# Fixing SyncE's order in a group-norm attention kernel, with loads and broadcasts tied to TensorE's progress

## Chip, cores and metric

One core of one Trainium2 chip runs the whole kernel. The metric is the device time of the program in microseconds, the median of three runs: 1814.81 us before the change (1812.54 to 1816.59).

## What is computed

The input x is 32 images of 256 channels and 32 x 32 places, all in 32-bit floats. The reference, cut to what matters:

```python
def _gn(v, G=32, eps=1e-5):           # group norm: 32 groups of 8 channels, no affine part
    ...
def attention(x):                      # xf: [b, 256, 1024]
    q = einsum('oc,bcs->bos', q_w, xf) + q_b
    kv = einsum('oc,bcs->bos', kv_w, xf) + kv_b
    k, v = kv[:, :256], kv[:, 256:]    # 8 heads of 32 channels
    mask = tril(ones(S, S), -1)        # strictly causal: a place sees only earlier ones
    scores = einsum('bhqd,bhkd->bhqk', q, k) / sqrt(32)
    scores = where(mask == 0, -10000, scores)
    attn = where(mask == 0, 0, softmax(scores))
    return einsum('bhqk,bhkd->bhqd', attn, v)
out = x + attention(_gn(x))
```

## The kernel before

The kernel goes through the 32 batches one after the other. A batch is worked in two groups of four heads (g), and each group in six "visits". So a batch has N = 12 visits, and the whole kernel has 384. In each visit TensorE makes scores for four heads (keys on partitions, queries along the free axis), ScalarE takes their exponentials, GpSimd masks the diagonal blocks, TensorE multiplies the exponentials of the visit before with the values, and VectorE adds exponentials up so that the softmax's sums can be formed later. Between these stand pieces of other batches' work: the projections of the next batch, the group norm of the one after, the division and the output of the one before.

Which piece stands at which visit is written out by hand. `when(i, f, where)` puts a function into one of three lists, and the main loop calls them at visit i: `at` after the scores have been issued, `between` after the values, `after` at the end of the visit. The tables PROJECT, PREPARE, SUMS, LOADS and FINISH hold the visit numbers, counted from the first visit of the batch concerned. The context `tc.manual_schedule(engines=...)` keeps this written order for the engines that it names: TensorE, ScalarE, VectorE and GpSimd. SyncE isn't among them, so the planner of the framework chooses the order of SyncE's instructions. SyncE does nothing but issue DMAs, and its queue is in order: an instruction that waits for a semaphore holds all behind it.

SyncE's DMAs in a batch, 256 KB each but for the inverses (32 KB):

- Four loads of x (`load_part`, L107), for the batch two later, quarter by quarter (two groups of channels, two halves of the places). Four buffers of x are kept; a buffer comes free when the batch that used it has been finished by VectorE.
- Four stacks (`stack`, L450): before each, GpSimd's queue folds a tile of partial sums twice with adding DMAs (`fold`, L444: 128 rows to 64 and 64 to 32, 512 KB and 256 KB in the profile's counting), and the stack copies the 32 rows into the tile `folded`. That tile has one buffer, which VectorE's `sum_folded` frees.
- One store of the inverses to DRAM (`invert`, L498), and four broadcasts of these from DRAM into the tile `rb`, 32 partitions for each head (`spread_inverses`, L505, at visits 8 to 11 of the next batch in the table). `rb` has one buffer.
- Four stores of the output (`finish`, L538). `finish` first multiplies the numerators with `rb` on VectorE (L530), adds bias and x (L532), writes the result into `rb` itself, and stores that.

The semaphore `bank_free` is already there. In `scores`, the last matmuls of the first part of a visit's scores each add one to it (four for a visit), and TensorE waits for the running total `live["free"]` before it writes the same banks of PSUM a second time:

```python
for ins in ends:
    ins.then_inc(bank_free, 1)
...
live["free"] = live.get("free", 0) + len(ends)
wait = nc.tensor.wait_ge(bank_free, live["free"])
```

The functions that the change touches and what calls them:

Of the kernel before, what the change touches and what calls it, by code (L numbers as in the profile page):

```python
# [14 lines left out]
ENG = mybir.EngineType  # L15
# [5 lines left out]
HALF = 512  # L21
# [11 lines left out]
def tile_norm_attention_residual(  # L33
# [19 lines left out]
    nc = tc.nc  # L53
# [4 lines left out]
    NH = S // HALF  # L58
# [6 lines left out]
    x_out = out.rearrange("b (g p) h w -> b p g (h w)", p=P)  # L65
# [15 lines left out]
        out=avg, in_=avg, pattern=[[-CPG, P // CPG], [0, CPG]],  # L81
# [3 lines left out]
        out=avg, in_=avg, pattern=[[CPG, P // CPG], [0, CPG]],  # L85
# [13 lines left out]
    def unshifted():  # L99
        live = {}  # L100
        bank_free = tc.alloc_semaphore("bank_free")
        xpool = tc.alloc_tile_pool(name="xpool", bufs=4)

        def load_part(b, g, cols):
            if (g, cols.start) == (0, 0):
                live["x", b] = xpool.tile([P, NG, S], F32, tag="x", name=f"x_{b}")
            nc.sync.dma_start(out=live["x", b][:, g, cols], in_=x_in[b, :, g, cols])  # L107
# [59 lines left out]
        def blocks(tokens, s, turned=False):  # L167

            of = tokens.rearrange("p (n s t) -> p n s t", s=2, t=P)[:, :, s, :]
            return of[:, :, ::-1] if turned else of  # L170
# [275 lines left out]
        def stack(b, n):  # L446
            if n == 0:
                live["folded", b] = work.tile([P, 4, HALF], F32, tag="folded", bufs=1, name=f"folded_{b}")
            total = live.pop(("sum", b, *divmod(n, NH)))
            nc.sync.dma_start(out=live["folded", b][n * HD : (n + 1) * HD], in_=total[:HD])  # L450
# [38 lines left out]
        def invert(b):  # L489
# [9 lines left out]
                out=spread.rearrange("a n j (m c) -> (n j m) a c", c=HD), in_=turned.rearrange("p (a c) -> p a c", a=2),  # L499
            )  # L500

        def spread_inverses(b, h):
            if h == 0:
                live["rb", b] = work.tile([P, 4, HALF], F32, tag="rb", bufs=1, name=f"rb_{b}")
            nc.sync.dma_start(  # L505
                out=live["rb", b][h * HD : (h + 1) * HD],
                in_=live["spread", b][h // 2, :, h % 2, :].unsqueeze(0).broadcast_to([HD, 4, HALF]),
            )
# [13 lines left out]
                inv.unsqueeze(2).broadcast_to([P, k, HD]),  # L522
            )

        def finish(b, n, within=slice(0, HALF)):
            g, hf = divmod(n, NH)
            cols = slice(hf * HALF + within.start, hf * HALF + within.stop)
            num, rb, xt = live["num", b, n], live["rb", b][:, n, within], live["x", b]
            num = num[:, within]
            nc.vector.tensor_mul(num, num, rb)  # L530
            for s in range(2):
                nc.vector.scalar_tensor_tensor(  # L532
                    blocks(rb, s), blocks(num, s, s == 1), v_bias_col[:, g : g + 1], blocks(xt[:, g, cols], s),
                    ALU.add, ALU.add,
                )
            if cols.start == 0:
                nc.vector.tensor_copy(rb[:, 0:1], xt[:, g, 0:1])
            nc.sync.dma_start(out=x_out[b, :, g, cols], in_=rb)  # L538

        def end_last(b):  # L540

# [27 lines left out]
        N, TOTAL = NG * len(VISITS), 2  # L569
# [40 lines left out]
        at, between, after = {}, {}, {}  # L610

        def when(i, f, where=at):
            where.setdefault(i, []).append(f)
# [15 lines left out]
        PROJECT = (-5, -4, -3, -2, -1, 0, 1, 2, 3, 4, 5, 6)  # L629
        PREPARE = (-12, -11, -9, -9, -8, -8, -7, -6, -5, -3)  # L630
        SUMS = (3, 7, 10, 13)
        LOADS = (7, 8, 11, 12)
        FINISH = (N + 13, N + 13, N + 14, N + 16)
        every = range(4)

        with tc.manual_schedule(engines={ENG.PE, ENG.Activation, ENG.DVE, ENG.Pool}):


            load_weights()
            if B > 1:  # L640
                load(1)
            junk = small.tile([P, 1], F32, tag="most", name="junk")
            nc.scalar.activation(junk, ones, AF.Exp)
            keep_busy(16)
            for g in range(NG):
                norm_channels(0, g)
            norm_mean(0)

            live["less_mean"] = work.tile([P, 4, HALF], F32, tag="folded", bufs=1, name="less_mean")[:, 0, :]
            for s in range(2):  # L650
                nc.scalar.activation(
                    blocks(live["less_mean"], s), blocks(live["x", 0][:, 1, :HALF], s, s == 1), AF.Identity,
                    bias=live["minus_mean", 0][:, 1:2],
                )
            turn_weights(0)
            norm_deviation(0)
            norm_variance(0)
            norm_rstd(0)
            for hf in range(NH):
                for g in range(NG):  # L660
                    norm_apply(0, hf, g)
                if hf == 0:
                    for n in (1, 2):
                        turn_weights(n)
                    keep_busy(3)
                    nc.vector.tensor_scalar_mul(qk_bias[:, 0, :], qk_bias[:, 0, :], SCALE)
            units = projections(0)
            for n, f in zip((None, None, None, 0, 0, 0) + PROJECT[6:], units):
                if n is None:
                    f()  # L670
                else:
                    when(n, f)
            if B > 1:
                prepare(1, (None, None, 0, 1, 2, 2, 3, 4, 5, 7))
            for b in range(B):
                first, last = b * N, b == B - 1
                if b >= 1:
                    for n, f in zip(PROJECT if not last else PROJECT[:-1] + (7,), projections(b)):
                        when(first + n, f)
                if b >= 2:  # L680
                    for n in range(NG * NH):
                        cols = slice(n % NH * HALF, (n % NH + 1) * HALF)
                        when(max(first - 2 * N + LOADS[n], 0), lambda b=b, n=n, cols=cols: load_part(b, n // NH, cols))
                    prepare(b, [(first + n,) if k in (2, 3) else first + n for k, n in enumerate(PREPARE)])
                if not last:
                    for n in every:
                        v = first + SUMS[n]
                        when(v, lambda b=b, n=n: fold(b, n, 2 * HD), after)
                        when(v + 2, lambda b=b, n=n: fold(b, n, HD), after)
                        when(v + 4, lambda b=b, n=n: stack(b, n))  # L690
                    late = b == B - 2
                    v = first + N + (5 if late else 6)
                    when(v, lambda b=b: sum_folded(b, every[:2]), after)
                    when(v + 1, lambda b=b: sum_folded(b, every[2:]), after)
                    when(v + 2, lambda b=b: invert(b))
                    for n in every:
                        when(v + 2 + (0 if late else n), lambda b=b, n=n: spread_inverses(b, n))
                    for n in every:
                        v = first + (N + 9 + n // 2 if late else FINISH[n])
                        when(v, lambda b=b, n=n: finish(b, n), after)  # L700
                else:
                    when(first + 3, lambda: sums(0, SUMMED[1], False), after)
                    when(first + 7, lambda: sums(1, SUMMED[5], False), after)
                    when(first + 9, lambda: sums(2, SUMMED[7], False), after)
                    when(first + 8, lambda b=b: invert_here(b, 0))
                    when(first + 9, lambda b=b: finish(b, 0))
                    when(first + 8, lambda b=b: invert_here(b, 1))
                    when(first + 8, lambda b=b: finish(b, 1))
                    when(first + 10, lambda b=b: invert_here(b, 2))
                    when(first + 11, lambda b=b: finish(b, 2), after)  # L710
            for i in range(B * N + 1):
                if i < B * N:
                    scores(*divmod(i, N))
                for f in at.pop(i, ()):
                    f()
                b, v = divmod(i - 1, N)
                if i == B * N:

                    sums(3, SUMMED[v], False)
                if i:  # L720
                    values(b, v)
                    for f in between.pop(i, ()):
                        f()
                    if b < B - 1 or v not in SUMMED or v == 1:
                        add_keys(b, v)
                if i in (B * N - 2, B * N - 1):

                    sums(3, SUMMED[v])
                for f in after.pop(i, ()):
                    f()  # L730
            assert not at and not between and not after
            outside = end_last(B - 1)
# [170 lines left out]
```

## Time and profile before

| What | Value |
|---|---|
| Runs | 1814.81 us median of three (1812.54 to 1816.59) |
| Profiled execution | 1814.37 us, of which the span from first to last instruction is 1812.7 us |
| TensorE matmuls | busy 1795.4 us (99%), 37036 of them, and as many weight loads |
| VectorE | busy 1674.0 us (92%) |
| ScalarE | busy 1457.5 us (80%) |
| GpSimd | busy 867.2 us (48%), the adding DMAs' issue included |
| DMA | 236.77 MB, mean 131 GB/s; SyncE's queue (q1) 28.0% of 16 engines' span, GpSimd's (q0) 35.7% |
| Granted TensorE clock | 0.999 |

Durations from issue to landing (medians): a broadcast `rb<-inverses` 4.7 us, a load of x 5.9 us, a store 5.4 us, the folds 4.9 to 6.9 us. A busy matmul row is modelled at its end, so that short pauses can hide in a TensorE that reads 99%; the length of a visit from the first matmul of its scores to the first of the next ones is exact. "issue" in the chain is time in which an engine waited for nothing that the profile shows. DMA-issuing instructions don't count as busy, so SyncE has no busy row; its timeline shows when each DMA was issued.

### The profile page before, as it was taken

The numbers are of one execution on the slowest core, as the hardware profiler recorded it, in microseconds if no ns is written. First come the engines' busy times: TensorE is split into PE (matmuls) and PEld (weight loads), VectorE is DVE, ScalarE is ACT, GpSimd is POOL, SyncE is SP. The second block draws the span as 40 slices with busy tenths as digits, with TensorE's granted clock in tenths as the row PEclk, the third lists the DMA queues.
The fourth block names the chain that finished last, engine by engine and source line by source line (L and its number), as shares of the span: only waits on it lengthen the run. The fifth ranks groups of instructions, "written<-read, shape, count | busy, mean of one in ns | idle before, by whom it ended". The sixth has DMA issues, their size and how long they took to land.

```text
span 1812.7 us, 81670 instructions
## 1 busy us (share of the span) xinstructions
PE 1795.4 (99%) x37036; PEld 954.8 (53%) x37036; DVE 1674.0 (92%) x1831; ACT 1457.5 (80%) x1985; POOL 867.2 (48%) x901
## 2 busy tenths in 40 slices
PE   9999999999999999999999999999999999999997
PEld 5555555555555555555555555555555555555553
DVE  4689999999999999999999999999999999999998
ACT  6888878888878888788887788887888878887774
POOL 2345454545554554545445545544454454544541
PEclk9999999999999999999999999999999999999999
DMA  3457676676766666666767666667667676676662
GB/s 124 72 96 141 138 140 121 134 151 126 148 123 136 140 140 139 136 126 134 150 127 147 124 137 137 139 134 136 126 137 144 131 142 117 136 154 120 124 114 84
DMA packets 86530, 236.77 MB, mean 131 GB/s; under 512 B 21280, under 2 KB 22304, under 8 KB 70304
## 3 DMA queue, kind: packets, MB, share of 16 engines
q0 software_dynamic: 15872, 97.53, 35.7%
q1 hardware_dynamic: 70304, 133.96, 28.0%
q8 instruction: 290, 4.75, 1.1%
q14 instruction: 64, 0.52, 0.1%
HBM read 66.85 MB, written 34.57 MB: 56 GB/s over the span
## 4 chain that ended last, share of the span: by engine, by line
PE 98%; DVE 1%; issue 0%; ACT 0%; DMA 0%; POOL 0%
PE sT L302 31%; PE acc L413 27%; PE pp L162 26%; PE ppv L162 13%; PE pd L465 1%; DMA x<-in_x_dram 0%; ACT e L388 0%; DVE st L177 0%; PE pv L162 0%; PE pm L162 0%; DVE rb_last L532 0%; ACT eh L384 0%; DVE rb_last L520 0%; DVE turned L517 0%; DVE acc L530 0%
## 5 line engine op out<-in xcount | busy, mean ns | idle before, releaser
L330 POOL TENSOR_SCALAR_AFFINE_SELECT diagonal<-eh 128x512 f32<-128x512 f32 x512 | 618.6, 1230 | 840.8 <-ACT eh L384 839.5
L388 ACT ACTIVATE e<-sT 128x1024 f32<-128x1024 f32 x768 | 744.6, 1022 | 252.9 <-PE sT L302 228.5
L431 DVE TENSOR_TENSOR e<-e,e 128x1024 f32<-128x1024 f32 x314 | 571.0, 1818 | 25.7 <-ACT v L266 4.2
L302 PE MATMUL sT<-q,k 32*64 32x128 f32 (+2 forms) x18432 | 587.5, 372 | 3.2 <-issue 2.5
L302 PEld LDWEIGHTS sT<-q,k 32*64 32x64 f32 x18432 | 397.1, 131 | 197.2 <-PE sT L302 69.6
L162 PE MATMUL pp<-xn,wT 128*32 128x512 f32 x4096 | 495.0, 598 | 1.1 <-issue 0.8
L413 PE MATMUL acc<-e,v 128*32 128x512 f32 (+3 forms) x4608 | 403.7, 450 | 0.0
L384 ACT ACTIVATE eh<-sT 128x768 f32<-128x768 f32 (+1 forms) x384 | 341.6, 890 | 0.0
L413 PEld LDWEIGHTS acc<-e,v 128*32 128x32 f32 x4608 | 150.4, 110 | 260.8 <-issue 238.6
L162 PE MATMUL ppv<-wT,xn 128*32 128x256 f32 x4096 | 247.8, 382 | 0.0
L162 PEld LDWEIGHTS pp<-xn,wT 128*32 128x32 f32 x4096 | 107.7, 109 | 199.7 <-issue 167.9
L431 DVE TENSOR_TENSOR diagonal<-diagonal,e 128x1536 f32<-128x1536 f32 x126 | 194.9, 1547 | 16.9 <-PE acc L413 9.2
L431 DVE TENSOR_TENSOR e<-e,eh 128x1024 f32<-128x1024 f32 x126 | 166.0, 1317 | 6.8 <-DVE e L431 0.5
L413 PEld LDWEIGHTS acc<-diagonal,v 128*32 128x32 f32 x4096 | 123.7, 110 | 85.9 <-issue 73.9
L431 DVE TENSOR_TENSOR e<-e,diagonal 128x2048 f32<-128x2048 f32 x63 | 144.2, 2289 | 21.7 <-POOL diagonal L330 21.6
L162 PEld LDWEIGHTS ppv<-wT,xn 128*32 128x32 f32 x4096 | 121.4, 109 | 78.7 <-issue 7.0
L413 PE MATMUL acc<-diagonal,v 128*32 128x128 f32 x4096 | 161.2, 273 | 0.0
L235 ACT ACTIVATE xn<-x,shift,rstd 128x256 f32<-128x256 f32 x248 | 136.8, 609 | 0.3 <-POOL shift L219 0.3
L444 POOL DMA_DIRECT2D diagonal<-diagonal x124 | 111.5, 900 | 35.1 <-DMA diagonal<-diagonal 35.1
L530 DVE TENSOR_TENSOR num<-num,rb 128x512 f32<-128x512 f32 x124 | 123.3, 994 | 0.6 <-DMA rb<-inverses 0.6
L532 DVE SCALAR_TENSOR_TENSOR rb<-num,v_bias_col,x 128x256 f32<-128x256 f32 x248 | 117.5, 515 | 4.4
L444 POOL DMA_DIRECT2D e<-e x124 | 102.2, 824 | 38.2 <-issue 38.2
(78 smaller groups left out, 983.3 us busy)
## 6 DMA issues: line engine op xcount, KB each, us to landing
diagonal<-diagonal POOLq DMA_DIRECT2D x62, 512.0 KB, 6.9
e<-e POOLq DMA_DIRECT2D x62, 512.0 KB, 5.3
rb<-inverses SPq DMA_DIRECT2D x124, 256.0 KB, 4.7
out_dram<-rb SPq DMA_DIRECT2D x124, 256.0 KB, 5.4
x<-in_x_dram SPq DMA_DIRECT2D x120, 256.0 KB, 5.9
diagonal<-diagonal POOLq DMA_DIRECT2D x62, 256.0 KB, 4.9
folded<-diagonal SPq DMA_DIRECT2D x62, 256.0 KB, 4.0
e<-e POOLq DMA_DIRECT2D x62, 256.0 KB, 5.4
```

What stands on the lines that cost most here:

```text
L162: nc.tensor.matmul(out[part], lhsT=lhsT[:, part], rhs=rhs, start=start, stop=stop, skip_group_check=True)
L235: nc.scalar.activation(to, of, AF.Identity, bias=live["shift", b][:, g : g + 1], scale=rstd)
L302: return nc.tensor.matmul(bank[c : c + KEYS, cols], lhsT=live["k", b, g][rows, kb * P + c : kb * P + c + KEYS], rhs=live["q", b, g][rows, ...
L330: nc.gpsimd.affine_select(out=square[:, :, place + s * P : place + (s + 1) * P], in_=raw[:, :, (1 - s) * KEYS : (3 - s) * KEYS], pattern=[ ...
L384: exp = nc.scalar.activation(eh.rearrange("p (n bank) q -> p bank n q", n=2)[:, :, :, :narrow], short[:, :, :, :narrow], AF.Exp)
L388: nc.scalar.activation(e[:, 2 * a : 2 * a + 2, :wide], pairs[a][:, :, :wide], AF.Exp)
L413: nc.tensor.matmul(acc[HD * j : HD * (j + 1), of], lhsT=live["v", b][:, kb, h * HD : (h + 1) * HD], rhs=e[:, j, :], start=first, stop=last ...
L431: nc.vector.tensor_add(to, to, tile_of(b, g, at))
L444: nc.gpsimd.dma_start(out=total[:rows], in_=total[rows : 2 * rows], accum_op=ALU.add)
L465: nc.tensor.matmul(pd[HD * j : HD * (j + 1), of], lhsT=pick, rhs=e[:, j, :], start=start, stop=stop, skip_group_check=True,)
L530: nc.vector.tensor_mul(num, num, rb)
L532: nc.vector.scalar_tensor_tensor(blocks(rb, s), blocks(num, s, s == 1), v_bias_col[:, g : g + 1], blocks(xt[:, g, cols], s), ALU.add, ALU.add,
```

## The change

SyncE is named in `manual_schedule`, so that its order is the written one. A new function `with_scores` makes SyncE wait on `bank_free` until the first part of the scores of the current visit (or of one `ahead` visits later) is done on TensorE. All four loads of a batch are now written at one visit (LOAD = 7 instead of 7, 8, 11 and 12): the first two behind the wait for visit 7, the others behind the wait for visit 8. The four broadcasts are written 2, 2, 3 and 4 visits after the inverses (instead of 0, 1, 2 and 3), and the last two stand behind a wait for the scores of their visit, which are visit 11 and visit 0 of the following batch. The four stores are written at the end of the visit after the one in which VectorE finishes. The stack with n = 0 is written at the end of its visit instead of behind its scores. Batch 30 (`late`) keeps its broadcasts and stores without waits, and batch 31 has its own ending.

```diff
+        def with_scores(ahead=0):
+            nc.sync.wait_ge(bank_free, live["free"] + 4 * ahead)
+
...
-        def finish(b, n, within=slice(0, HALF)):
+        def finish(b, n, within=slice(0, HALF), later=None):
...
-            nc.sync.dma_start(out=x_out[b, :, g, cols], in_=rb)
+            send = lambda: nc.sync.dma_start(out=x_out[b, :, g, cols], in_=rb)
+            if later is None:
+                send()
+            else:
+                later(send)
...
-        LOADS = (7, 8, 11, 12)
+        LOAD = 7
+        SPREAD = (2, 2, 3, 4)
...
-        with tc.manual_schedule(engines={ENG.PE, ENG.Activation, ENG.DVE, ENG.Pool}):
+        with tc.manual_schedule(engines={ENG.PE, ENG.Activation, ENG.DVE, ENG.Pool, ENG.SP}):
...
-                        when(max(first - 2 * N + LOADS[n], 0), lambda b=b, n=n, cols=cols: load_part(b, n // NH, cols))
+                        v = max(first - 2 * N + LOAD, 0)
+                        if n % NH == 0:
+                            when(v, lambda n=n: with_scores(n // NH))
+                        when(v, lambda b=b, n=n, cols=cols: load_part(b, n // NH, cols))
...
-                        when(v + 4, lambda b=b, n=n: stack(b, n))
+                        when(v + 4, lambda b=b, n=n: stack(b, n), at if n else after)
...
-                        when(v + 2 + (0 if late else n), lambda b=b, n=n: spread_inverses(b, n))
+                        at_visit = v + 2 + (0 if late else SPREAD[n])
+                        if not late and n > 1:
+                            when(at_visit, with_scores)
+                        when(at_visit, lambda b=b, n=n: spread_inverses(b, n))
...
-                        when(v, lambda b=b, n=n: finish(b, n), after)
+                        later = None if late else lambda send, v=v: when(v + 1, send, after)
+                        when(v, lambda b=b, n=n, later=later: finish(b, n, later=later), after)
```

## Prediction

> **What bounds the kernel now.** I read the page first: engine totals, the chain, the DMA queues.
>
> ```profile
> PE 1795.4 (99%) x37036; PEld 954.8 (53%) x37036; DVE 1674.0 (92%) x1831; ACT 1457.5 (80%) x1985; POOL 867.2 (48%) x901
> PE 98%; DVE 1%; issue 0%; ACT 0%; DMA 0%; POOL 0%
> q8 instruction: 290, 4.75, 1.1%
> ```
>
> TensorE is busy for 99% of the span and carries 98% of the chain. No DMA of SyncE is on the chain. So the change can only gain where TensorE, looking busy, loses time. I therefore asked for the windows of each visit, batch by batch. Visit 0 takes 4.57 us at best. The first two lines below are visit 0 of batches 3 and 23, the third is the sum over visit 0 of batches 1 to 30, the last the sum over visits 4 and 5 of the same batches (undisturbed: 9.24 us a pair).
>
> ```profile
> 184.39:188.96 4.57, 4.57 (x109) 2.32 (x106) 4.36 (x3) 3.22 (x4) 0.67 (x1) 1.00 0.69 149
> 1293.17:1298.55 5.38, 4.95 (x108) 2.42 (x104) 5.14 (x4) 3.44 (x4) 1.27 (x2) 1.00 0.60 126
> sum 145.31, PE 143.44 PEld 70.67 DVE 137.81 ACT 97.95 POOL 27.75; mean PE 4.78 PEld 2.36 DVE 4.59 ACT 3.26 POOL 0.93
> sum 283.89, PE 281.85 PEld 159.14 DVE 276.23 ACT 212.40 POOL 230.98; mean PE 9.39 PEld 5.30 DVE 9.21 ACT 7.08 POOL 7.70
> ```
>
> Visit 0 loses 145.31 - 30 x 4.57 = **8.2 us**, visits 4 and 5 lose 283.89 - 30 x 9.24 = **6.7 us**. Every other visit repeats to about 0.02 us in all these batches, and an undisturbed batch is 55.09 us (batches 1, 2, 3, 26 and 30). About 15 us is all there is to win in the steady part. What is the loss? The chain around the start of batch 23:
>
> ```profile
> 1293.24 1.25 PE sT L302 x35
> 1294.50 0.43 issue
> 1294.93 0.55 PE sT L302 x9
> ```
>
> TensorE stands in the middle of the scores with no semaphore to blame. The DMA records of the window 1292.3 to 1293.6 hold one packet of the instruction queue, which starts at 1292.35 and ends at 1293.5. TensorE goes on 1.44 us after that end. I compared all 11 recorded pauses of 0.1 us or more at visits 0, 4 and 5: each ends 1.2 to 1.6 us after such a packet. TensorE runs out of instructions, because their transfer starts late. What it waits behind is in SyncE's timeline:
>
> ```profile
> 1262.50 0.51 SPq L450 DMA_DIRECT2D folded<-e  x1
> 1265.54 0.33 SPq L538 DMA_DIRECT2D out_dram<-rb  x1
> 1265.92 1.97 SPq L107 DMA_DIRECT2D x<-in_x_dram  x4
> 1280.15 0.51 SPq L450 DMA_DIRECT2D folded<-diagonal  x1
> 1282.09 0.38 SPq L498 DMA_DIRECT2D inverses<-inv_turned  x1
> 1284.87 1.76 SPq L505 DMA_DIRECT2D rb<-inverses  x4
> 1293.50 0.52 SPq L450 DMA_DIRECT2D folded<-e  x1
> ```
>
> Batch 22 begins at 1238.05. Four broadcasts of 256 KB leave together at 46.8 to 48.2 us into it, and land at 50.5, 51.8, 53.0 and 54.3 us: 1.25 us each, one behind the other. GpSimd's fold (e<-e, issued at 49.0) stands behind them. The fetch starts at 54.3.
>
> **What the skill says.** The Trainium skill, "Runtime: NRT & Kernel Launch", section Instruction fetch mechanics: instructions come in blocks of 16 KiB (256 of them) over a DMA queue of the sequencer's own, and crossing a block is mostly hidden. The trace agrees on the size: 2 x 37036 / 256 = 289.3 blocks, and 290 packets. "Mostly hidden" fails here for 15 us. "DMA: Bandwidth & Descriptors", section Queues, rings and completion order, says that each DMA engine takes turns between queues packet by packet, so that a fetch should pass a long copy quickly. The trace is otherwise: the fetch waits for what was queued before it. I follow the trace. A batch has 2304 matmuls and weight loads, exactly nine blocks, which is why the same visits suffer each time.
>
> **Part by part**, in microseconds into a batch (visits 7, 8 and 11 start at 32.2, 36.7 and 50.5).
>
> *Order of SyncE fixed.* In the trace the order of a batch is: stack 1 at 0.0, stack 2, stores 0, 1, 2, stack 3, store 3, four loads, stack 0, inverses, four broadcasts. The written order of after is the same, but for the last two broadcasts: broadcast 2 before stack 1, broadcast 3 after it. No other transfer is overtaken: cost 0, as long as the head of the queue isn't late.
>
> *Stores a visit later.* SyncE already waits for VectorE before each store (11.7, 13.2, 20.0, 27.6), and their places in the order stay. Being written a visit later changes nothing: 0. If they do go later, at most a visit (4.6 us) each, they have 20 us until rb is written again; bound: 2 us either way through visits 4 and 5, taken at 0.
>
> *Waits.* Four on SyncE per batch, tens of ns each (its semaphore instructions at L505 take 17 to 28 ns), 0 on TensorE. Behind the wait for visit 7 (SyncE idle from 28 to about 32.7) stand the loads and stack 0, which goes at 42.1, when VectorE frees its tile. Behind that for visit 11 (47.6 to about 51.0) stand broadcast 2 and stack 1, whose fold lands at 54.8 now. Behind that for the next visit 0 (to about 0.7) stand broadcast 3 and stack 2, due at 10.7.
>
> *Loads.* 120 of 256 KB move from 27.8-29.4 to about 32.7, 33.2, 37.3 and 37.8 (the first scores are done some 0.4 to 0.6 after their visit begins, an estimate from 1.4 us for all 48). They take 5.9 us, so the last lands by 44. VectorE reads them 7.2 us into the next batch, at 62: 18 us to spare, cost 0. The fetch that starts at 34 to 35.6 now is relieved, but no visit loses there: gain 0.
>
> *Broadcasts 2 and 3.* 60 of them move, to 51.0 and 0.7. Before the fetch then lie two broadcasts and GpSimd's fold instead of four and the fold: 2 x 1.25 = 2.5 us less. It starts at 54.3 - 2.5 = 51.8 in batch 22, where the loss of 0.81 says that 53.5 is early enough. The largest loss of all is 0.81, so 2.5 us covers every batch: **-8.2 us, and -0.57 in batch 31 (5.14 instead of 4.57)**. Could broadcast 3 now hold the first fetch of a batch? Unhindered, that starts at 0.6 to 1.1; the broadcast's packets come no sooner than 1.4. If it does, 1.25 us are added to starts of 1.8 to 4.0, where about 4.3 to 6.0 is early enough (an estimate from where TensorE ran dry elsewhere): 0. VectorE needs all broadcasts at 8.7 to 9.6; broadcast 3 lands at 0.7 + 4.7 = 5.4, at worst 0.7 + 6.7 = 7.4: 0.
>
> *Visits 4 and 5.* Nothing moves in 11 to 30 us. But of the batches with under 0.2 us lost at visit 0, one of twelve has its fetch at visit 4 late (start from 23.6), and of those with over 0.3, nine of fourteen. A pause at visit 0 moves GpSimd's next fold (10.1 to 10.6) onto the stack at 10.7; they interleave and push two fetches back. Without the pause I take four fifths of the loss away: **-5.4 us**; ends 0 and -6.7.
>
> Sum: -8.2 - 0.6 - 5.4 = -14.2. The profiled execution took 1814.37 (span 1812.7 and 1.7 around it), so 1800.2; the median of the runs is 0.44 higher, so **1800.5 us**.
>
> **Rivals.** (a) Only visit 0 is cured, visits 4 and 5 have their own cause: -8.8, **1806**. For it: batch 25 loses nothing at visit 0 and 0.67 later. Against: nine of fourteen to one of twelve. (b) The fetch at visit 0 is still held, by GpSimd's fold or by broadcast 2, which comes at 51.7 when a fetch unhindered starts at 50.6 to 51.1; what was gained is lost again: **1813 to 1816**. (c) Slower: loads 2 and 3 reach the DMA engines at about 38.0 and 38.5, GpSimd's 512 KB fold at 38.9, and the unhindered fetch starts at 37.2 to 38.2. If it comes behind all three (1.25 + 1.25 + about 2.5), it starts near 43, where 41.1 to 42.8 is early enough. At 1 us a batch that is 30 us against 14 gained: **1830**. The point that decides is 0.47 us a batch, a start near 42.5. Against it: the fetch would have to come behind the fold as well. (d) It doesn't do what it says: SyncE's order was already this one, and the waits pass at once. The trace denies it: the broadcasts leave at 48, long before visit 11.
>
> **Numbers.** Main case (both places cured, 1797.5 to 1803) 0.52; (a), 1803 to 1808.5, 0.26; between that and no change 0.03; (b) and (d) 0.09; (c) and late data on VectorE 0.10. Within 0.2% (3.6 us) is what a measurement of this kernel can't tell from no change. Faster 0.81, same 0.09, slower 0.10. The range takes in the main case and (a).
>
> **What would show it.** Right: visit 0 at 4.57 in all batches, broadcasts 2 and 3 at about 51 and 0.7, instruction packets near the end of a batch at 51 to 52.5, visits 4 and 5 at 9.24 in most batches, stores where they were. Wrong: a pause marked "issue" in visits 8 to 10 or 0, an unchanged sum at visits 4 and 5, or VectorE waiting for rb.

## The result, and the profile after

The changed kernel takes **1802.67 us** in the median of five runs (1800.82 to 1804.72). The kernel before, on the same chip, takes 1814.81 (1812.54 to 1819.09). The ratio is 0.993, with an interval of 0.9913 to 0.9947: 12.1 us less, where 14.3 were predicted. The profiled execution took 1802.24 us with a span of 1800.5; before it was 1814.37 and 1812.7.

First the page of after: busy time of the engines, the queue of instruction fetches, and the shares of the chain.

```profile
PE 1787.0 (99%) x37036; PEld 952.8 (53%) x37036; DVE 1672.6 (93%) x1831; ACT 1455.7 (81%) x1985; POOL 872.0 (48%) x901
q8 instruction: 290, 4.75, 1.1%
PE 98%; DVE 1%; ACT 0%; DMA 0%; issue 0%; POOL 0%
```

The counts of instructions are those of before, and so are the 290 instruction packets. TensorE's "busy" time has fallen by 8.4 us with not one matmul fewer: as was said of its row above, short pauses can be counted as busy. The page alone doesn't show where the time came from. The windows do. The first line is the sum over visit 0 of batches 1 to 30, the second that over visits 4 and 5:

```profile
sum 137.26, PE 137.26 PEld 69.44 DVE 130.57 ACT 96.49 POOL 20.01; mean PE 4.58 PEld 2.31 DVE 4.35 ACT 3.22 POOL 0.67
sum 281.36, PE 280.76 PEld 158.37 DVE 273.79 ACT 211.86 POOL 229.56; mean PE 9.36 PEld 5.28 DVE 9.13 ACT 7.06 POOL 7.65
```

Against before, visit 0 gained 145.31 - 137.26 = **8.05 us** and visits 4 and 5 gained 283.89 - 281.36 = **2.53 us**. Batch 31, up to the scores of its last visit, gained 0.87 (53.09 to 52.22), the start 0.10, and what comes after those scores 0.49. Together that is 12.04 of the 12.13 by which the two profiled executions differ; the rest is spread over the other visits. The loss that remains is 0.16 us at visit 0 and 4.2 us at visits 4 and 5 (281.36 - 30 x 9.24), in batches 5, 15, 17, 21, 23, 25 and 29 (0.16 to 1.21 us each). No other visit loses more than 0.05 us in its sum over the 30 batches.

The chain of waits at the start of batch 23, where the kernel before had its row of 0.43 us marked "issue":

```profile
1286.81 1.30 PE acc L413 x24
1288.10 1.42 PE sT L302 x51
1289.52 1.85 PE pp L162 x16
```

All the scores of visit 0 now stand in one row. Visit 4 of the same batch still has its pause, in the middle of the scores as before:

```profile
1306.45 1.39 PE sT L302 x36
1307.84 0.29 issue
1308.13 0.33 PE sT L302 x4
```

SyncE's timeline of batch 22 and the start of batch 23 (batches begin at 1232.94 and 1288.03; columns are start, length, source line, operation, count). The broadcast is now L510 and the store L543:

```profile
1265.84 6.23 SPq L107 DMA_DIRECT2D x<-in_x_dram  x4
1275.00 0.51 SPq L450 DMA_DIRECT2D folded<-diagonal  x1
1276.94 0.38 SPq L498 DMA_DIRECT2D inverses<-inv_turned  x1
1281.03 3.51 SPq L510 DMA_DIRECT2D rb<-inverses  x3
1287.25 0.52 SPq L450 DMA_DIRECT2D folded<-e  x1
1288.78 0.64 SPq L510 DMA_DIRECT2D rb<-inverses  x1
1298.84 0.51 SPq L450 DMA_DIRECT2D folded<-diagonal  x1
1299.74 8.64 SPq L543 DMA_DIRECT2D out_dram<-rb  x3
```

The loads go 32.9 us into the batch and later. The row of three broadcasts runs from 48.1 to 51.6, since the third waits in it; the fourth goes 0.75 into the next batch. In the medians over batches 2 to 29 the four go at 47.3, 47.7, 51.3 and 0.75. The stores still go 11.7 us into a batch and later.

Medians over batches 2 to 29, in microseconds into a batch, from the DMA records of the two traces:

| | before | after |
|---|---|---|
| inverses landed | 47.0 | 47.3 |
| the four broadcasts landed | 50.5, 51.8, 53.1, 54.3 | 50.8, 51.9, 56.0, 61.9 |
| GpSimd's fold issued, landed | 49.3, 55.3 | 49.0, 53.7 |
| instruction fetch for the end of the batch starts | 54.30 | 53.15 |
| instruction fetch for visits 4 and 5 starts | 17.43 | 16.87 |

The fetch that visit 0 depends on starts 1.15 us earlier, which is enough there. SyncE's own waits, in us in total, times and the longest in us, show that its new waits are long and cost nothing:

```profile
SPq L505 <- PE sT L302: 434.6, 115, 45.7
```

SyncE stands for 434.6 us behind TensorE's scores, while TensorE isn't held: every visit but 0, 4 and 5 keeps its length.

### The profile page after: what moved, and what is told of

Read it like the earlier page. It is cut to its first block, busy times and chain, and to the rows that moved or that the text cites. A ratio compares the mean times of both kernels' runs of the same rounds, so it can differ in the third digit from the quotient of the medians.

```text
span 1800.5 us, 81787 instructions
## 1 busy us (share of the span) xinstructions
PE 1787.0 (99%) x37036; PEld 952.8 (53%) x37036; DVE 1672.6 (93%) x1831; ACT 1455.7 (81%) x1985; POOL 872.0 (48%) x901
## 4 chain that ended last, share of the span: by engine, by line
PE 98%; DVE 1%; ACT 0%; DMA 0%; issue 0%; POOL 0%
PE sT L302 31%; PE acc L413 28%; PE pp L162 26%; PE ppv L162 13%; PE pd L465 1%; DMA x<-in_x_dram 0%; ACT e L388 0%; DVE st L177 0%; PE pv L162 0%; PE pm L162 0%; DVE rb_last L537 0%; ACT eh L384 0%; DVE rb_last L525 0%; DVE turned L522 0%; DVE acc L535 0%
## 5 line engine op out<-in xcount | busy, mean ns | idle before, releaser
L431 DVE TENSOR_TENSOR e<-e,e 128x1024 f32<-128x1024 f32 x314 | 571.7, 1821 | 24.5 <-ACT v L266 3.2
L302 PE MATMUL sT<-q,k 32*64 32x128 f32 (+2 forms) x18432 | 579.9, 372 | 0.7 <-issue 0.5
```

Source lines behind the costliest of these rows:

```text
L302: return nc.tensor.matmul(bank[c : c + KEYS, cols], lhsT=live["k", b, g][rows, kb * P + c : kb * P + c + KEYS], rhs=live["q", b, g][rows, ...
L431: nc.vector.tensor_add(to, to, tile_of(b, g, at))
```

## Experiments: which part of the change does what

In all of them "V0" is the loss at visit 0 and "V45" that at visits 4 and 5, in batches 1 to 30 of the profiled execution, against undisturbed sums of 137.1 and 277.2 us. Before has 8.2 and 6.7, after 0.2 and 4.2. Each kernel ran beside the kernel before; the ratio is to that. A profile is one execution: where a kernel's times scatter, V0 and V45 scatter too.

The first four ran together. Before had a median of 1814.81 there, in 19 runs from 1809.41 to 1820.38.

**1. The broadcasts go together again, all else as after.**

```diff
-        SPREAD = (2, 2, 3, 4)
+        SPREAD = (0, 0, 0, 0)
...
-                        if not late and n > 1:
-                            when(at_visit, with_scores)
```

> The changed kernel, but all four broadcasts leave together behind the inverses, as before the change; the late loads stay. Theory A (the broadcasts in front of the fetch cost visit 0): visit 0 of batches 1 to 30 loses about 8 us again, the time is 1810 to 1813 us. Theory B (the loads' moving gave the gain): visit 0 stays below 1 us of loss, the time is 1802 to 1804. Visits 4 and 5: if pauses at visit 0 cause their loss it goes back to about 6.7; if they have their own cause it stays near 4.

Measured: 1829.14 us (1823.79 to 1835.85), ratio 1.0076 (1.0058 to 1.0095). That is *slower than before*. Visit 0, and visits 4 and 5:

```profile
sum 161.41, PE 148.23 PEld 72.11 DVE 151.70 ACT 100.20 POOL 35.44; mean PE 4.94 PEld 2.40 DVE 5.06 ACT 3.34 POOL 1.18
sum 290.49, PE 285.79 PEld 160.09 DVE 282.83 ACT 214.92 POOL 232.27; mean PE 9.53 PEld 5.34 DVE 9.43 ACT 7.16 POOL 7.74
```

V0 is 24.3, V45 is 13.3. The profiled execution was the slowest of the six, so these losses are at the upper end. Of V0, 5.9 us fall in batch 13 alone, whose chain reads:

```profile
743.27 2.56 issue
745.83 0.50 PE sT L302 x9
746.34 3.64 PE pp L162 x16
749.98 2.42 PE acc L413 x24
```

The pause is only 2.6 us of the 5.9. Behind it the same work takes about twice as long as in after (1.85 and 1.30 us above): the granted clock of TensorE is 0.5 from 745.3 to 752.1 us. It is the only such drop between the first batch and the last in any of these profiles, and it makes up the other 3.3 us.

```profile
745.83:749.98 4.15, 4.15 (x30) 1.30 (x33) 4.01 (x5) 1.73 (x2) 1.73 (x2) 0.50 0.13 30
```

(The last three numbers are the granted clock, the busy share of the DMA engines and GB/s.) In the medians over batches 2 to 29 the inverses land at 48.25 us into the batch, the last of the four broadcasts at 55.6, and the fetch starts at 55.30. Theory B is refuted; of theory A the place of the loss came, but the size was three times the 8 us expected.

**2. The loads are not held, all else as after.**

```diff
-                        if n % NH == 0:
-                            when(v, lambda n=n: with_scores(n // NH))
```

> The changed kernel without the two waits of the loads, which then leave behind store 3 at about 28 us into a batch, as before the change. Theory A: visit 0 loses under 1 us, the time is 1801 to 1804 us. Theory B: visit 0 loses about 8 us again, 1810 to 1813.

Measured: 1801.69 us (1799.51 to 1803.68), ratio 0.9929 (0.9913 to 0.9944), the same as after. Visit 0 and visits 4 and 5:

```profile
sum 137.20, PE 137.20 PEld 69.61 DVE 130.38 ACT 96.57 POOL 19.88; mean PE 4.57 PEld 2.32 DVE 4.35 ACT 3.22 POOL 0.66
sum 282.38, PE 280.94 PEld 157.23 DVE 274.82 ACT 212.17 POOL 230.96; mean PE 9.36 PEld 5.24 DVE 9.16 ACT 7.07 POOL 7.70
```

V0 is 0.1 and V45 5.2. The fetch starts at 53.13, as in after. The waits in front of the loads bring nothing once the broadcasts wait.

**3. Only the order and the later stores; neither loads nor broadcasts wait.** The edits of 1 and 2 together.

> The changed kernel without any of the four waits a batch, and with the broadcasts together: only SyncE's order is written out. Theory A: like the kernel before, 1812 to 1817 us, visit 0 loses about 8. Theory C (the written order alone gave the gain): 1802 to 1804.

Measured: 1815.38 us (1809.76 to 1819.31, 14 runs), ratio 1.0001 (0.9988 to 1.0014). In the profile visit 0 and visits 4 and 5 read:

```profile
sum 142.30, PE 140.86 PEld 70.58 DVE 135.01 ACT 97.38 POOL 24.96; mean PE 4.70 PEld 2.35 DVE 4.50 ACT 3.25 POOL 0.83
sum 290.65, PE 286.32 PEld 162.09 DVE 282.86 ACT 215.00 POOL 231.81; mean PE 9.54 PEld 5.40 DVE 9.43 ACT 7.17 POOL 7.73
```

V0 is 5.2 and V45 13.5: less lost than in before at the one, more at the other, and 1.5 us are lost at visits 7 and 8. This profile was the slowest of the 14 runs, 3.9 us above their median. The four medians make a table of two by two:

| | broadcasts together | broadcasts 2 and 3 wait |
|---|---|---|
| loads not held | 1815.4 (3) | 1801.7 (2) |
| loads wait | 1829.1 (1) | 1802.7 (after) |

The wait of two broadcasts is worth 14 us without the loads' wait and 26 with it, and the wait of the loads by itself *costs* 14 us. How it does is read from the traces of 1 and 3 and wasn't tested alone. With the loads held, the inverses land 1.4 us later (48.25 against 46.85) and the whole group of broadcasts goes later. With the broadcasts still together, the fetch starts at 55.30 instead of 54.06. Part of this is the loads' own doing: with only two broadcasts in the group, holding the loads makes the inverses land 0.6 us later (47.32 in after, 46.72 in 2). The other part may be the pauses acting on themselves, since in 1 the inverses are also issued 0.6 later than in 3 (44.75 against 44.12). When only two broadcasts leave, the lateness of 0.6 does no harm: the fetch starts at 53.15 in after and at 53.13 in 2.

**4. After, with the first two stores held until the scores of visit 3.**

```diff
-                later(send)
+                later((lambda: (with_scores(1), send())) if n == 0 else send)
```

> The changed kernel, and stores 0 and 1 wait in addition for the first scores of visit 3 (about 13.9 us into a batch, instead of 11.7 and 13.2). If what is left at visits 4 and 5 (4.2 us) comes from the fetch of about 14 us that stands behind these stores: that fetch starts near 15.5 instead of 16 to 18, the loss at visits 4 and 5 falls below 1 us, the time is 1798 to 1800 us. If the fetch stands behind the fold and the stack alone: no change, 1802 to 1804.

Measured: 1798.67 us (1798.33 to 1798.89), ratio 0.9914 (0.9899 to 0.9929). The stores go at 14.1 and 14.5 instead of 11.7 and 13.2, the fetch for visits 4 and 5 starts at 16.15 instead of 16.87, and V45 is gone:

```profile
sum 277.18, PE 277.18 PEld 153.92 DVE 269.62 ACT 210.21 POOL 228.89; mean PE 9.24 PEld 5.13 DVE 8.99 ACT 7.01 POOL 7.63
```

V0 is 0.50. So the loss at visits 4 and 5 is a transfer's doing as well: what stands in front of that fetch includes the first two stores.

**5. Are the pauses the borders of instruction blocks?** The kernel before, with 32 matmuls of one column put ahead of everything. The page counts 64 more matmuls and 64 more weight loads: 128 instructions, half a block.

```diff
+        def shift_blocks(n):
+            pt = ps_s.tile([P, 2, HALF], F32, tag="sT", name="shift_blocks")
+            for _ in range(n):
+                nc.tensor.matmul(pt[0:1, 0, 0:1], lhsT=ident[:, 0:1], rhs=ident[:, 0:1], start=True, stop=True)
...
+            shift_blocks(32)
```

> The kernel before, with 32 one-column matmuls more at the start (128 instructions of TensorE, half a block of 256; their result isn't used). Everything after keeps its work, only the borders of the instruction blocks fall half a block, about 3 us, earlier in each batch. Theory F (the pauses are late instruction blocks): the 8 us lost at visit 0 and the 7 us at visits 4 and 5 leave these visits; what is lost at all is lost at others. Rival (the pauses belong to the work of these visits: a bank, a weight load, a tile): visits 0, 4 and 5 lose 8 and 7 us as before. The start grows by some us.

Measured, a single run: 1805.18 us, span 1803.4. Its visits 0, 1, 4 and 5, and 6, in this order:

```profile
sum 137.10, PE 137.10 PEld 69.55 DVE 130.48 ACT 96.58 POOL 19.84; mean PE 4.57 PEld 2.32 DVE 4.35 ACT 3.22 POOL 0.66
sum 139.17, PE 139.04 PEld 73.88 DVE 127.36 ACT 114.16 POOL 90.01; mean PE 4.63 PEld 2.46 DVE 4.25 ACT 3.81 POOL 3.00
sum 277.17, PE 277.17 PEld 153.91 DVE 269.61 ACT 210.29 POOL 229.19; mean PE 9.24 PEld 5.13 DVE 8.99 ACT 7.01 POOL 7.64
sum 140.23, PE 138.76 PEld 70.23 DVE 134.15 ACT 127.66 POOL 47.50; mean PE 4.63 PEld 2.34 DVE 4.47 ACT 4.26 POOL 1.58
```

Without a single change to any DMA, visit 0 and visits 4 and 5 are without loss, and new losses stand at visit 1 (139.17 - 136.80 = 2.37) and visit 6 (140.23 - 137.10 = 3.13). The pauses change their place with the instruction count, with other fetches late now that the borders have shifted by half a block. The place of the pauses in the instruction stream says the same. Count all of TensorE's recorded instructions from the start, its sequencer's included, and take as a pause each jump of over 0.2 us in the start of a matmul against its earliest place in the same visit. In before, TensorE goes on at instruction 193 or 194 of a block of 256 after 21 of 24 such pauses; here it does so at 190 to 193 after all six, though they stand 128 instructions further in. TensorE resumes 1.2 to 1.6 us after the end of an instruction packet in those 21, and 1.3 to 1.6 in these six. That shows that the pauses belong to the borders of instruction blocks and not to the visits' own work or data.

**6. A whole block of shift, in after** (64 such matmuls; 256 instructions). V45 in the profile of after falls on odd batches alone. A batch has nine blocks, so the parity of a block's number goes with the parity of the batch; a shift by one block exchanges them.

> The changed kernel, with 64 one-column matmuls more at the start (256 instructions, one whole block; their result isn't used). The borders fall where they fell, but each block has a number higher by one. In the changed kernel the late fetches at visit 4 are all in odd batches (3, 5, 9, 15, 17, 23, 25). Theory G (blocks of even number, fetched at about 14 us, come about 0.8 us later than odd ones, as if they were served elsewhere): the late ones are now in even batches, visit 0 keeps under 1 us of loss. Rival (odd batches themselves differ, by buffers used in turn): they stay odd.

Measured, a single run: 1809.88 us, 3.65 more than after at the start, where the small matmuls stand and the granted clock is 0.5 from 11.4 to 14.8 us. V0 is 0.0, and visits 4 and 5 lose 8.2:

```profile
sum 285.44, PE 283.64 PEld 159.77 DVE 277.85 ACT 213.91 POOL 230.69; mean PE 9.45 PEld 5.33 DVE 9.26 ACT 7.13 POOL 7.69
```

The lossy batches are 5, 11, 13, 15, 19, 21, 22, 23, 27 and 29: odd, but for one. That it is the number of the block is refuted.

**7. After, with the stores written at once, as before the change.**

```diff
-                        later = None if late else lambda send, v=v: when(v + 1, send, after)
+                        later = None
```

> The changed kernel, but each store is written at the visit in which VectorE finishes, as before the change; all waits stay. By the prediction (the stores wait for VectorE anyway): no change, 1801.5 to 1804 us, stores at 11.7, 13.2, 20.0 and 27.5 us into a batch in both. If writing them a visit later had part in the gain: 1806 or more.

Measured: 1797.53 us (1797.14 to 1798.36), ratio 0.9918 (0.9904 to 0.9931; before 1813.24 in 12 runs, 1810.36 to 1818.15). That is neither of the two times expected: the median lies 5.1 us below that of after, on another chip (11 and 12 below set them side by side). Visits 4 and 5:

```profile
sum 277.12, PE 277.12 PEld 153.89 DVE 269.91 ACT 210.28 POOL 229.53; mean PE 9.24 PEld 5.13 DVE 9.00 ACT 7.01 POOL 7.65
```

V45 is 0 and V0 is 0.33. The reason stands in SyncE's timeline (batch 23 starts at 1286.03):

```profile
1297.74 1.87 SPq L543 DMA_DIRECT2D out_dram<-rb  x2
1299.72 1.17 SPq L450 DMA_DIRECT2D folded<-diagonal  x1
1306.41 7.77 SPq L543 DMA_DIRECT2D out_dram<-rb  x2
1314.28 0.94 SPq L450 DMA_DIRECT2D folded<-e  x1
```

The stores go at 11.7 as ever, since VectorE sets that. But stack 2 now stands *behind* them in SyncE's queue and goes at 13.7 instead of 10.9, and the fetch starts at 16.2. In after, stack 2, store 0 and store 1 leave between 10.8 and 13.2. Stack 3 goes later too (27.9 instead of 24.5, behind store 3), but no visit shows a change there. It is enough to move either the stores (4) or stack 2 (7) out of this group.

**8. Only the order, with the first two stores held** (the edit of 3 with that of 4).

> The kernel with SyncE's order alone written out (no waits of loads and broadcasts), and stores 0 and 1 waiting for visit 3. If visits 4 and 5 are held by the stores alone, whatever happens at visit 0: their loss falls from 13 to under 2 us, visit 0 keeps its 5 to 8, the time is 1803 to 1807 us. If pauses at visit 0 cause it (the prediction's step): over 5 us stay at visits 4 and 5, 1808 or more.

Measured: 1807.72 us (1806.29 to 1811.43), ratio 0.9972 (0.9961 to 0.9984). Visit 0, and visits 4 and 5:

```profile
sum 143.80, PE 142.47 PEld 70.93 DVE 136.42 ACT 97.63 POOL 26.31; mean PE 4.75 PEld 2.36 DVE 4.55 ACT 3.25 POOL 0.88
sum 277.70, PE 277.70 PEld 154.28 DVE 270.14 ACT 210.28 POOL 229.70; mean PE 9.26 PEld 5.14 DVE 9.00 ACT 7.01 POOL 7.66
```

V0 stays, at 6.7, and V45 is down to 0.5; the time lies 0.7 us above the range expected for that. The pauses at visit 0 don't by themselves make those at visits 4 and 5. Each has its own transfers in front of its own fetch. That they add to them isn't excluded: as long as the stack and the first two stores leave together, the profiles with losses at visit 0 have a V45 of 6.7, 13.3 and 13.5 (before, 1, 3), those with under 0.4 us lost there 4.2 to 8.2 (after, 2, 6, 9, 11).

**9. Is it the place of the output in DRAM?** Store 1 lands 0.85 us later in odd batches than in even ones (19.76 against 18.91 in after). Here neighbouring batches exchange the places of their outputs, so the output is in another order than the reference's.

```diff
-            send = lambda: nc.sync.dma_start(out=x_out[b, :, g, cols], in_=rb)
+            send = lambda: nc.sync.dma_start(out=x_out[b ^ 1, :, g, cols], in_=rb)
```

> The changed kernel, but each batch is stored in its neighbour's place of the output (0 in 1, 1 in 0, and so on), so that odd batches are written to even addresses of 1 MB. In the changed kernel store 1 lands 0.85 us later in odd batches (19.76 against 18.91 us into the batch, means), and only odd ones have the late fetch at visit 4. If the address in DRAM makes the difference: the late ones are now even, and store 1 lands later in these. If something else in SBUF or in the program alternates: they stay odd.

Measured, a single run: 1804.37 us. V45 is 5.3. The losses of 0.1 us and more are still all in odd batches (11, 13, 15, 17, 21, 23, 25, 29), and store 1 still lands later in odd ones (19.92 against 18.94). The address of the output isn't the cause. What alternates from batch to batch stays open.

**10. Stores at once and loads not held** (7 with 2): of after, the fixed order, the loads' one visit, the wait of two broadcasts and the place of stack 0 are left.

> The changed kernel with the stores written at once (so that stack 2 leaves behind stores 0 and 1) and without the waits of the loads; of the change there remain SyncE's written order and the waits of the last two broadcasts. If the waits of the loads are of no use: 1797 to 1798.5 us, as with the stores at once alone; visit 0 and visits 4 and 5 together lose under 1 us. If they protect a fetch: 1800 or more.

Measured: 1798.21 us (1797.15 to 1798.95), ratio 0.9907 (0.9892 to 0.9922; before 1816.54 in 9 runs, 1811.24 to 1818.40). V0 and V45 are both 0.0, and 0.5 us is lost at visit 8. It can't be told from 7: with the stores at once the loads' waits bring nothing either.

**11 and 12. After and experiment 7 beside each other**, unchanged, since they had run on different chips. The best version is thereby measured against after itself.

> The changed kernel itself, run beside the version with the stores written at once, so that the two are compared on one chip, and to see how its loss at visits 4 and 5 repeats. If the place of stack 2 among the first two stores is what costs visits 4 and 5: 1801 to 1805 us, visits 4 and 5 lose 4 to 6 us in the profiled execution, visit 0 under 0.5. If its 4.2 us of loss was one execution's scatter and the versions are alike: within 1.5 us of the other kernel, loss under 1 us.

> The stores written at once, beside the changed kernel. If the place of stack 2 behind the first two stores is worth what the separate runs showed (5.1 us): 1797 to 1799 us, no loss at visits 4 and 5, 4 to 6 us below the changed kernel, its times within 1.5 us of each other. If the two are alike: within 1.5 us of the changed kernel, 1801 or more.

Measured: after 1800.88 us (1799.97 to 1804.54, ratio to before 0.9936, 0.9921 to 0.9952), stores at once 1797.91 us (1797.27 to 1798.10, ratio 0.9919, 0.9904 to 0.9935), six runs each; before 1813.18 in 11 runs. The gap is 3.0 us, less than the 4 to 6 expected, but no run of the one reaches into those of the other. Visits 4 and 5 of after, then visit 0 and visits 4 and 5 of the version with the stores at once:

```profile
sum 282.90, PE 281.69 PEld 158.98 DVE 275.35 ACT 212.54 POOL 230.40; mean PE 9.39 PEld 5.30 DVE 9.18 ACT 7.08 POOL 7.68
sum 137.10, PE 137.10 PEld 69.48 DVE 130.45 ACT 96.55 POOL 19.81; mean PE 4.57 PEld 2.32 DVE 4.35 ACT 3.22 POOL 0.66
sum 277.14, PE 277.14 PEld 153.90 DVE 269.92 ACT 210.27 POOL 229.50; mean PE 9.24 PEld 5.13 DVE 9.00 ACT 7.01 POOL 7.65
```

The profiled execution of after was its slowest (1804.54), with 5.7 us lost at visits 4 and 5. The other version loses nothing in any visit of batches 1 to 30. In this profile of after, batch 16 (0.87) is among the lossy ones beside odd ones from 13 to 29, so the rule of the odd batches is a tendency.

## Why the prediction was right or wrong, point by point

**The total.** -14.2 was predicted for the profiled execution, -12.1 came. Against the terms of the sum, visit 0 stood 0.15 us short, batch 31 0.30 better and visits 4 and 5 2.9 short; 0.66 that no term had came from the start (0.10), the end (0.49) and scattered remainders. So the total is nearer than its parts: the 2.9 missing at visits 4 and 5 was in part made up by about 1 us that the sum didn't foresee, and that is luck.

**What bounds the kernel: right.** The gain in batches 1 to 30 lies in the visits where TensorE had stood without instructions, and no other visit became shorter. Experiment 5 shows the kind of pause without any DMA being moved. The Trainium skill ("Runtime: NRT & Kernel Launch", section Instruction fetch mechanics) gives 16 KiB blocks of 256 instructions, and this case agrees: a shift by 128 instructions moved every loss (5), and a shift by 256 left them at visits 4 and 5 (6). "Mostly hidden", which the prediction held against that page, is a matter of counting: in the trace of before, 30 visits hold a pause of 0.1 us or more, against 290 fetches.

**Visit 0: the size right, the working off.** -8.05 against -8.2. That the waits of broadcasts 2 and 3 bring it is shown by experiments 1 to 3. But the fetch was to come 2 x 1.25 = 2.5 us earlier, and it came 1.15 us earlier (54.30 to 53.15). The mis-sized term is GpSimd's fold. In before it landed at 55.3, after the broadcasts; in after it lands at 53.7, and the fetch starts 0.5 us ahead of that. Taking two broadcasts away let the fold move up into part of their place. That it is the fold which holds the fetch now is read from these times and wasn't tested alone. It was enough because the largest loss was 0.81, and 53.5 had been early enough: the size came out by the margin in the working, not by its 2.5.

**Batch 31: too low.** -0.87 instead of -0.57. Its visit 0 gave what was worked out (5.14 to 4.57); the other 0.30 lies in its later visits, for which the prediction has no term (0.50 gained at visit 4, 0.20 lost at visit 1).

**Visits 4 and 5: wrong.** -2.5 instead of -5.4. The step that failed is the inference from one batch in twelve against nine in fourteen: that a pause at visit 0 pushes later fetches back. Experiment 8 keeps the pauses at visit 0 (6.7) and has almost none at visits 4 and 5 (0.5). The part of rival (a) that was set aside, "visits 4 and 5 have their own cause", was right. That cause, without which hardly anything is lost there, is the group of stack 2, store 0 and store 1 between 10.8 and 13.2 (4 and 7). After left this group as it was, so most of the 6.7 had no reason to go. The 2.5 that did go may be what the pauses at visit 0 had added, or scatter between executions, for a second profile of after lost 5.7 there (11), and 2, with the same stores, lost 5.2; this stays open.

**Order of SyncE, 0: right as a sum, for a reason too narrow.** Order and later stores alone make 1.0001 (3). But the profile of 3 has less at visit 0 and more at visits 4 and 5, so two opposite shifts may lie in that.

**Stores a visit later, 0: not a nothing.** The times of the stores stayed, as predicted. Yet the place in the written order decides what SyncE may issue ahead of them: written at once, they hold stack 2 back by 2.8 us, and that is worth 3.0 us side by side (11 and 12). The prediction asked when the stores go, and not what they keep waiting.

**Waits on SyncE, 0: right.** They stand for 434.6 us and hold nothing that TensorE needs.

**Loads, 0: right only beside the other edit.** With the broadcasts waiting, it is nothing (2 against after). By itself the same edit costs 14 us (1 against 3), because the inverses and the whole group behind the loads come later. The 18 us to spare was the loads' own margin. The margin of what stands behind them in the queue was the one that counted.

**Broadcast 3 late for VectorE, 0: right.** It lands at 61.9 - 55.1 = 6.8 us into the batch, within the predicted 5.4 to 7.4, and no wait of VectorE on `rb` is in the trace.

**Rivals.** (b) was half right: GpSimd's fold does seem to hold the fetch still. But the fold itself now lands earlier, so that what was gained wasn't lost again; the 1.15 us and V0 at 0.2 exclude its 1813 to 1816. (c), losses at visits 8 to 10, didn't come: these visits have their undisturbed length in batches 1 to 30 of after. A slower kernel by way of the loads did exist, but through visit 0 and only without the broadcasts' wait (1). (d) is excluded by the timeline. (a)'s time, 1806, is 3 us above what came.

## What to carry to other kernels

When an engine that reads 99% busy stands for tenths of a microsecond with nothing released, look for the instruction queue's packets just before (here most of the pauses end 1.2 to 1.7 us after one) and for what was issued in the few microseconds ahead of them. Then move one transfer out of that group, and shift the instruction count by half a block in a second kernel to see whether the pauses change their place. An in-order DMA queue has to be priced by what an instruction keeps waiting behind it as much as by its own time: here a stack that went 2.8 us later was worth 3 us, and loads with 18 us to spare cost 14 when their lateness was passed on. And two edits that touch the same few microseconds must be tried as two by two, since one of them was worth nothing or minus 14 us according to the other.

## What the runs showed of the hardware that was not expected

- A fetch can lose to earlier transfers by microseconds. The Trainium skill ("DMA: Bandwidth & Descriptors", section Queues, rings and completion order) has each DMA engine take turns between queues, a whole packet at a time. That a fetch should therefore pass a long copy quickly was the prediction's own conclusion. In these runs the start of the fetch followed what had been queued ahead of it, at 53.1 to 53.2 with two broadcasts in front (after, 2, 4, 7, 9, 11) and at 54.0 to 55.3 with four (before, 1, 3, 8).
- The lead of a fetch is about one block, an estimate from the trace of before. In the 21 pauses counted under experiment 5, the packet that has just landed brings the block at whose first instruction TensorE goes on. Counted so, the earliest fetches start 240 to 300 instructions ahead of need at seven of a batch's nine places, and 180 to 200 at the two on which visits 0 and 4 depend. A block lasts 6.1 us on average (55.09 / 9).
- Kernels with more of these pauses scatter more. Before ranges over 11.0 us in 19 runs, and experiment 1 over 12.1 in 6. Experiments 4, 7, 10 and 12, with under 1 us of pauses left, range over 0.6, 1.2, 1.8 and 0.8 us in 5 or 6.
- Store 1 lands 0.85 us later in odd batches (0.98 in experiment 9, 0.82 in before), and most losses at visits 4 and 5 fall in those. With stack 2 behind the stores (7) the gap is only 0.18 us. It is neither the number of the instruction block (6) nor the output's place (9), and stays open.
- A late fetch can cost more than its pause. After the 2.6 us without instructions in experiment 1 the granted clock was 0.5 for 6.8 us, and another 3.3 us were lost. It happened once, 2.0 us after TensorE had stopped. Shorter pauses, up to 1.7 us in the same run, left the clock at 1.0.
